# Expert tiles of three sequences computed beside the last sequence's attention, later rows by a second list of four tiles

## The chip, the cores and the metric

The kernel runs on one core of a Trainium2 chip. The metric is the time of one execution on the device in microseconds (us); lower is better. A core has a matrix engine (TensorE, PE in the profile, with its weight loads under PEld), a vector engine (VectorE, DVE), a scalar engine (ScalarE, ACT), a general engine (GpSimd, POOL) and a sync engine (SyncE, SP) that mostly issues DMA transfers. POOL and ACT issue transfers too; a transfer whose addresses come from a tensor (an indirect DMA) is issued by POOL. Each engine works off its own list of instructions in order, and the engines wait for each other by semaphores.

## The reference

Four sequences (B = 4) of 1024 tokens, 256 features each, in float32, go through four blocks, each added onto its input after a layer norm: a gated recurrence, a mixture of 8 experts, causal attention with 16 heads of 64, and a mixture of 32 experts. The change touches the last block, and where the third one ends.

```python
z = jnp.einsum('dvh,bhcv->bcd', W, y) * (math.sqrt(d_embed / d_value) / num_heads)   # end of attention
...
X = x.reshape(-1, D)                                   # 4096 tokens, normalised
logits = (X @ gate_w.T).astype(jnp.float32)
scores = jax.nn.sigmoid(logits)
_, idx = jax.lax.top_k(scores + bias[None, :], K)      # K = 4 of E = 32 experts
w = jnp.take_along_axis(scores, idx, axis=-1)
w = w / jnp.clip(jnp.sum(w, axis=-1, keepdims=True), 1e-12, None)
eid = idx.reshape(-1)
onehot = (eid[:, None] == jnp.arange(E)[None, :]).astype(jnp.int32)
pos = jnp.take_along_axis(jnp.cumsum(onehot, axis=0) - 1, eid[:, None], axis=1)[:, 0]
valid = pos < C                                        # C = 256 rows for each expert
posc = jnp.minimum(pos, C - 1)
xe = jnp.zeros((E, C, D), x.dtype).at[eid, posc].add(jnp.where(valid[:, None], Xrep, jnp.zeros((), x.dtype)))
h = jax.nn.silu(jnp.einsum('ecd,edi->eci', xe, W1)) * jnp.einsum('ecd,edi->eci', xe, W3)
ye = jnp.einsum('eci,eid->ecd', h, W2)
gflat = jnp.where(valid, w.reshape(-1), jnp.zeros((), x.dtype))
yrows = ye[eid, posc] * gflat[:, None]                 # 0 where not valid
out = yrows.reshape(-1, K, D).sum(axis=1)
out = out + jax.nn.silu(X @ sw1.T) * (X @ sw3.T) @ sw2.T     # the shared expert
```

Two things matter. An expert takes only its first 256 entries, in the order of the tokens over all four sequences; later ones count as zero. And `bias` is drawn with a spread of 2, next to scores between 0 and 1, so that nearly every token asks for the same few experts, which the first tokens fill.

## The kernel before, in words

**Slots.** The expert block has 32 x 256 = 8192 slots (`NSLOT`), in 64 slot tiles of 128 rows. `xs_d` in device memory holds one row for each slot (and 128 rows of zeros behind them): the 256 features, their mean and rstd, the four slots that the token has, and the number of the token. `yt_d` holds four result rows for each token. Both are filled with zeros early in attention (`l4_zeros`).

**Routing** (`l4_route(b, h, ...)`, one half of a sequence, 512 tokens): statistics and a layer norm on VectorE, transposes and scores on TensorE, the four best by `max` and `match_replace`, positions by a matmul with a triangular matrix plus the running count (`runs1`), and then 16 indirect scatters (`to_slots`, four k times four tiles of tokens) that POOL issues to write the rows into `xs_d`. For the last sequence only the four scatters with k = 0 are issued at once; the others are kept in the list `late`. `second` keeps, for each half sequence, whether any token has a second valid slot. The first half of the shared expert is computed at the end of `l4_route`, the second half in `l4_shared`, which adds it onto `x`. The gates go to `gates1`.

**Scatters.** The class `Scatters` lets eight indirect scatters be on their way; a reader of the target (`wait`) waits for the last eight sent.

**Attention** is one loop, `run_steps`, over 192 steps: 4 sequences x 8 pairs of heads x 6 steps. The order of the instructions in it is written out by hand (`manual_schedule`): in each step score matmuls, the row minimum on VectorE, exponents on ScalarE (tiles `pe`, eight buffers), transposes and the weighted sum. Other work is woven in by the class `Beside`: a list of jobs, each a Python generator, done one after the other. A job yields "pe" ahead of matmuls, "post" ahead of what reads their result, and "dve" ahead of VectorE work. In a step's three places for side work, matmuls of the job can stand where the list `side` says "beside"; at the end of each step there are 1 to 3 ticks (`TICKS`) for "dve" pieces. While sequence b is in attention, the jobs are: the output projection of sequence b-1 (`l3_out`, matmuls `pz`), the layer norm of sequence b+1, then routing (both halves) and `l4_shared` (both halves) of sequence b-1.

The attention weights behind the first pair of heads are loaded in three transfers of 896 KB each into `wq_t`, `wk_t` and `wv_t`.

**The tail.** Behind the loop come `l3_out` and both halves of `l4_route` of the last sequence; from here on the build's scheduler chooses the order on each engine, under the data dependencies. Then the pool `l4_mid` opens, in space that attention's pools leave, and the expert block is done:

- the count of rows of each expert, `taken1` (which of the 64 slot tiles have rows), a running sum over it (`upto`), and `l4_list(0, 16)`: the numbers of the first 16 occupied tiles, by comparing the running sum with 0 to 15 over 16 x 64 elements; entries beyond the last occupied tile point to the zeros
- a branch (`If`) that issues the `late` scatters if the last sequence has second slots
- `l4_tiles(0, 16)`: for each entry POOL loads the expert's weights (`ew`, 384 KB, by a number read from the list) and SP the tile's rows (`xg`); then normalise (VectorE), transpose (TensorE), copy (ScalarE), two products, SiLU, the third product, a copy, and an indirect scatter of the 128 results to `yt_d` (`to_tokens`)
- a branch that does the other 48 tiles, if more than 16 are occupied
- `l4_shared` of the last sequence
- the results: for each of the 32 tiles of tokens a load `yg` from `yt_d` on SP (`l4_take`) and additions on VectorE (`l4_add`: x + gate * yg); four additions for each tile of the first sequence (all four k), one for the others, 56 in all. Three branches, one for each sequence behind the first, stand between them for second slots. The stores go out on ACT's queue: eight for the first sequence, two for each of the others.

## Time and profile before

| what | value |
|---|---|
| time, median of 7 runs | 2190.59 us (2187.34 to 2197.59) |
| the profiled execution's own time | 2193.18 us |
| its span | 2191.5 us |
| mean granted TensorE clock in it | 0.923 |
| busy share PE / PEld / DVE / ACT / POOL | 86% / 56% / 57% / 44% / 12% |
| moved by DMA | 109.22 MB |
| end of attention (last weighted sums) | 2029.5 us |
| end of `l3_out` of the last sequence | 2057.4 us |
| end of its routing, scatters included | 2092 us |
| first load of slot rows (`xg`) | 2098.36 us |
| first load of results (`yg`) | 2147.69 us |

The profile is one execution, taken by the hardware profiler. Times inside it are microseconds from the start of its span. A row of the timeline has start, length, engine, line and operation; "x16" behind it means that 16 instructions of the kind are drawn together. SPq and POOLq are the times at which an engine's queue issued transfers. The granted clock is the share of full speed at which TensorE was let run in a stretch. Busy shares are averages over the whole span; the stages in the table differ much from them.

### The profile page before, as it was taken

To read this page: it belongs to the slowest core of one execution; us is meant where nothing else is said; L and a number is where in the kernel's file an instruction comes from. 1 tells how busy PE (TensorE), PEld (TensorE's weight loads), DVE (VectorE), ACT (ScalarE), POOL (GpSimd) and SP (SyncE) were. 2 spreads that over 40 slices of the span, in tenths; PEclk is the share of its full clock that TensorE was granted. 3 is DMA by queue.
4 is the path that set the end of the run, shared out by engine and by line. 5 is a ranking of instruction groups with operands and counts; after the bars stand their busy time and mean duration, and the time that the engine had idled before them with its cause. 6 is when DMAs were issued, how large, how long until landed. Compare 5 with 4: busy or idle time off the path is not lost. (4 is left out here: it accounts for less than half of the span.)

```text
span 2191.5 us, 45014 instructions
## 1 busy us (share of the span) xinstructions
PE 1877.4 (86%) x17488; PEld 1221.3 (56%) x17488; DVE 1245.9 (57%) x4059; ACT 965.3 (44%) x2511; POOL 267.7 (12%) x307
## 2 busy tenths in 40 slices
PE   5567699999999999999989799998969988978761
PEld 2435356665656666766646456664546655656541
DVE  6585222244237776647748564774756557656554
ACT  3253122222246666645546453654635345546020
POOL 0233300022012100000020200002020020110040
PEclk9577899999999999999989899998989998989875
DMA  8112211122134423000000000000000000000056
GB/s 326 39 58 73 76 44 49 44 80 77 45 117 146 152 99 122 2 1 2 2 21 2 2 2 2 2 2 2 2 1 2 2 2 2 2 1 2 2 177 212
DMA packets 82351, 109.22 MB, mean 50 GB/s; under 512 B 13646, under 2 KB 71082, under 8 KB 80976
## 3 DMA queue, kind: packets, MB, share of 16 engines
q1 hardware_dynamic: 61632, 73.40, 10.0%
q0 software_dynamic: 15168, 27.05, 4.0%
q10 hardware_dynamic: 5328, 5.78, 0.8%
q8 instruction: 142, 2.33, 0.4%
q14 instruction: 81, 0.66, 0.1%
HBM read 51.75 MB, written 64.77 MB: 53 GB/s over the span
## 5 line engine op out<-in xcount | busy, mean ns | idle before, releaser
L1302 ACT ACTIVATE pe<-ps,nm 128x512 f32<-128x512 f32 (+3 forms) x768 | 438.6, 580 | 263.0 <-DVE nm L1289 252.0
L1323 PE MATMUL pt<-ident,pe 64*128 64x64 f32 x4608 | 254.5, 231 | 91.6 <-issue 31.0
L1359 PE MATMUL pa<-pT,v 128*64 128x128 f32 (+1 forms) x4096 | 325.9, 291 | 3.1 <-issue 3.0
L1323 PEld LDWEIGHTS pt<-ident,pe 64*128 64x128 f32 x4608 | 212.3, 141 | 185.4 <-issue 88.6
L1273 PE MATMUL ps<-k,q 64*128 64x512 f32 (+3 forms) x1536 | 307.4, 507 | 3.6 <-issue 3.5
L1359 PEld LDWEIGHTS pa<-pT,v 128*64 128x64 f32 x4096 | 242.9, 138 | 105.8 <-issue 88.1
L1344 ACT COPY pT<-pt 128x512 f32<-128x512 f32 (+2 forms) x384 | 179.2, 520 | 195.0 <-PE pt L1323 172.3
L604 PE MATMUL ph<-w_t,xgT 128*128 x544 | 257.6, 615 | 7.3 <-DVE desc_C L528 5.8
L1287 DVE TENSOR_REDUCE nm<-ps 128x1 f32<-128x512 f32 x256 | 175.9, 687 | 153.7 <-PE ps L1273 124.8
L849 POOL DMA_INDIRECT xs_d<-x,row_l x104 | 102.6, 987 | 1249.0 <-DVE second L1001 1066.1
L1273 PEld LDWEIGHTS ps<-k,q 64*128 64x128 f32 x1536 | 138.4, 191 | 75.4 <-issue 63.7
L1344 DVE COPY pT<-pt 128x256 f32<-128x256 f32 (+3 forms) x384 | 178.4, 506 | 2.3 <-PE pt L1323 1.3
L1289 DVE CUSTOM_DVE_ANT_0 ps<-ps,mask_a,nm 128x128 f32<-128x128 f32 (+3 forms) x256 | 143.2, 559 | 40.0 <-DVE nm L1287 8.9
L604 PEld LDWEIGHTS ph<-w_t,xgT 128*128 128x128 f32 x544 | 101.0, 197 | 110.7 <-issue 102.3
L1302 ACT ACTIVATION_READ_ACCUMULATOR pe<-ps,nm 128x1 f32 x768 | 153.9, 200 | 0.0
L893 PE MATMUL pq<-l_xT,wq_t 128*64 128x512 f32 x448 | 112.1, 622 | 26.6 <-ACT pe L1302 25.1
L1289 DVE CUSTOM_DVE_ANT_0 ps<-ps,mask_a 128x128 f32<-128x128 f32 (+3 forms) x256 | 119.8, 517 | 23.2 <-PE ps L1273 21.7
L893 PE MATMUL pz<-wo_t,y 128*64 128x256 f32 x1024 | 115.0, 379 | 0.0
L893 PE MATMUL pv<-wv_t,l_xT 128*64 128x128 f32 x1792 | 111.5, 278 | 2.9 <-ACT pe L1302 2.9
L624 PE MATMUL py<-w_t,hidT 128*128 x464 | 109.6, 379 | 0.0
L893 PE MATMUL pk<-l_xT,wk_t 128*64 128x512 f32 x448 | 107.2, 599 | 1.1 <-ACT pe L1302 1.1
L893 PEld LDWEIGHTS pv<-wv_t,l_xT 128*64 128x64 f32 x1792 | 100.7, 140 | 5.6 <-ACT pe L1302 3.6
(370 smaller groups left out, 2201.8 us busy)
## 6 DMA issues: line engine op xcount, KB each, us to landing
yt_d<-zeros SPq DMA_DIRECT2D x32, 512.0 KB
xg<-xe_d SPq DMA_DIRECT2D x68, 129.0 KB
yq_d<-ys SPq DMA_DIRECT2D x68, 128.0 KB
xs_d<-zeros SPq DMA_DIRECT2D x65, 131.5 KB
w_t<-w_dram SPq DMA_DIRECT2D x8, 1024.0 KB
ew<-e_w_dram POOLq DMA_DIRECT2D x16, 384.0 KB
x<-x_in_dram SPq DMA_DIRECT2D x8, 512.0 KB
w_t<-w_dram SPq DMA_DIRECT2D x8, 512.0 KB
```

What stands on the lines that cost most here:

```text
L604: nc.tensor.matmul(pt, xgT[:, c, :], w[:, c, k * H0 : (k + 1) * H0], start=(c == 0), stop=(c == NC_ - 1),)
L624: nc.tensor.matmul(py, hidT[:, c, :], w[:, c, :], start=(c == 0), stop=(c == H0 // P - 1))
L849: i = nc.gpsimd.indirect_dma_start(out=self.out, out_offset=bass.IndirectOffsetOnAxis(ap=idx, axis=0), in_=src, in_offset=None, bounds_che ...
L893: nc.tensor.matmul(out[r], lhsT[:, r], rhs, start=start, stop=stop)
L1273: nc.tensor.matmul(t[:, :n], qs[b, p][rows, i * P : (i + 1) * P], ks[b, p][rows, kc * 512 : kc * 512 + n], start=True, stop=True,)
L1287: nc.vector.tensor_reduce(m[:, 0:1], t, AX.X, ALU.min)
L1289: nc.vector.tensor_tensor_reduce(out=t[:, :n], in0=t[:, :n], in1=mask[:, 512 - n :], scale=1.0, scalar=-LOWEST if kc == 0 else m[:, 0:1], ...
L1302: inst = nc.scalar.activation(pe[:, :n], sps.pop((u, k, par))[:, :n], AF.Exp, bias=ms[u, i, par][:, 1:2], scale=-1.0, accum_out=ls[b, p][: ...
L1323: nc.tensor.transpose(pts[u][r][:, j, par, :], pes[u, k, par][rows, j * P : (j + 1) * P], ident[rows, rows],)
L1344: copy(to, pts[u][r][:, :n])
L1359: nc.tensor.matmul(pas[0][rows, cols], vs[b, p][:, j, rows], pTs[u][:, j, par, a * P :], start=(j == 0), stop=(j == nb - 1),)
```

## The change

1. A new job, `l4_experts_beside`, is appended for `Beside` behind the jobs that run during the last sequence's attention. It waits until the loop has reached the third pair of heads from the end (pair 29 of 0 to 31), by then counts the rows of sequences 0 to 2, makes a list of 12 slot tiles (`NL_A`) and computes these tiles two at a time, in the places that `Beside` has, with results scattered to `yt_d`. What is not done when the loop ends is done behind it, ahead of `l3_out` of the last sequence. Its working space is the buffer of normalised inputs that would belong to a fifth sequence (`room4`), and the attention weights of pairs that are done: `w_pairs[:, 0]` is scratch for the list, `w_pairs[:, 1]` to `[:, 4]` hold expert weights.
2. For that, the attention weights get a new layout, pair by pair, and come in 21 transfers of 128 KB instead of three of 896 KB.
3. `floors` keeps, for each tile that was done, how many rows it had. `owner` holds the number of the last sequence's first result row for these tiles. `over1` says whether more than 12 tiles were occupied.
4. In the tail the list now has 4 entries (`NL_B`), for tiles in which rows came in beyond `floors`. `l4_list` with `first_row` has two more passes to fetch each entry's `owner`, and `l4_rows` has two more operations, which turn away (send out of range) the results of rows that belong to earlier sequences.
5. The loads, additions and stores of sequences 0 to 2 now stand ahead of the tail's first branch and of the four tiles; for sequences 1 and 2 with the first k only. Behind the four tiles and `l4_shared` come eight loads and additions and two stores of the last sequence.
6. The five branches become two, on one flag (`more`): more than 12 tiles at first, more than 4 tiles later, or a second slot in any token behind sequence 0. In the second, all other tiles, additions and stores are done over.
7. SiLU in the expert tiles is worked out with Tanh and two VectorE operations, as the shared expert does it.
8. The buffers of `pe` go from eight to seven. The iotas `tile_t` and `entry` move to the block's setup, early in the kernel.

The new job and its helpers, and the core of the rest (`...` stands for lines left out):

```diff
+NL_A, NL_B = 12, 4
...
+    def l4_keys(flat, name):
+        upto = l4s.tile([P, NL], F32, name=f"upto_{name}", tag="upto")
+        nc.vector.tensor_tensor_scan(upto, ones[:, :NL], flat, 0.0, ALU.mult, ALU.add)
+        key = l4s.tile([P, NL], F32, name=f"key_{name}", tag="key")
+        nc.vector.tensor_mul(key, upto, flat)
+        nc.vector.tensor_scalar(key, key, -1.0, None, ALU.add)
+        return upto, key
+
+    def l4_list(key, j0, n, eq, first_row=None):
+        eq = eq.rearrange("p (n t) -> p n t", t=NL)
+        nc.vector.tensor_tensor(
+            eq, key.unsqueeze(1).to_broadcast([P, n, NL]),
+            entry[:, j0 : j0 + n].unsqueeze(2).to_broadcast([P, n, NL]), ALU.is_equal,
+        )
+        rows = None
+        if first_row is not None:
+            own = l4s.tile([P, 16, NL], F32, name=f"own_{nm}", tag="xT1")[:, :n]
+            nc.vector.tensor_mul(own, eq, first_row.unsqueeze(1).to_broadcast([P, n, NL]))
+            rows = l4s.tile([P, 16], F32, name=f"rows_{nm}", tag="lrows")[:, :n]
+            nc.vector.tensor_reduce(rows, own, AX.X, ALU.add)
+        nc.vector.tensor_mul(eq, eq, tile_t.unsqueeze(1).to_broadcast([P, n, NL]))
+        t = l4s.tile([P, 16], F32, name=f"list_{nm}", tag="list")[:, :n]
+        nc.vector.tensor_reduce(t, eq, AX.X, ALU.add)
...
+        return first, e, slot, rows
+
+    def l4_load(k, lst, xg, w):
+        first, e, slot, rows = lst
+        ev = nc.values_load(
+            e[0:1, k : k + 1], engines=[mybir.EngineType.Pool], min_val=0, max_val=E1 - 1,
...
+        )
+        nc.gpsimd.dma_start(out=w, in_=e_w[bass.ds(ev, 1)].rearrange("o p a i -> p (o a) i"))
+        rv = nc.values_load(
+            first[0:1, k : k + 1], engines=[mybir.EngineType.SP], min_val=0, max_val=NSLOT,
...
+        )
+        to_slots.wait(nc.sync.dma_start(out=xg, in_=xs_d[bass.ds(rv, P), :]).ins)
+
+    def l4_rows(name, xg, slot, row, pool, bufs):
+        nc.vector.tensor_scalar(
+            xg[:, :D], xg[:, :D], xg[:, D : D + 1], xg[:, D + 1 : D + 2], ALU.subtract, ALU.mult
+        )
+        eq = pool.tile([P, K1], F32, name=f"heq_{name}", tag="heq", bufs=bufs)
+        nc.vector.scalar_tensor_tensor(
+            eq, xg[:, D + 2 : D + 2 + K1], slot, choice, ALU.is_equal, ALU.mult
+        )
+        to = pool.tile([P, 1], F32, name=f"to_{name}", tag="to", bufs=bufs)
+        nc.vector.tensor_reduce(to, eq, AX.X, ALU.add)
+        if row is not None:
+            old = pool.tile([P, 1], F32, name=f"old_{name}", tag="old", bufs=bufs)
+            nc.vector.tensor_scalar(old, xg[:, XP - 1 : XP], row, float(FAR), ALU.is_lt, ALU.mult)
+            nc.vector.tensor_add(to, to, old)
+        to_i = pool.tile([P, 1], I32, name=f"to_i_{name}", tag="to_i", bufs=2 * bufs)
+        nc.vector.scalar_tensor_tensor(to_i, to, float(FAR), xg[:, XP - 1 : XP], ALU.add, ALU.add)
+        return to_i
+
+    def l4_experts_beside(sm, ps, tag, w_of, ready):
+        while not ready():
+            yield "dve"
+        room = xtp.tile([P, NC_ * S], F32, name="room4", tag="xT")
...
+        yield "pe"
+        pn = ps.tile([P, E1], F32, name="pn_a", tag=tag)
+        for par in range(2):
+            r = slice(par * DH, (par + 1) * DH)
+            nc.tensor.matmul(pn[r], ones[:, r], runs1[-1][:, NT // 2, :], start=True, stop=True)
+        yield "post"
...
+        yield "dve"
...
+        yield "dve"
...
+        yield "dve"
+        lst = l4_list(key, 0, NL_A, w_of(0).rearrange("p a c m -> p (a c m)"))
+        yield "dve"
...
+        for j in range(2):
+            l4_load(j, lst, xgs[j % 2], weights(j))
+        for j0 in range(0, NL_A, 2):
+            for j in js:
+                yield "dve"
+                tos.append(l4_rows(f"a{j}", xgs[j % 2], lst[2][:, j : j + 1], None, l4s, 1))
+            yield "pe"
...
+            yield "post"
+            nc.scalar.copy(xgT, pt)
+            if j0 + 2 < NL_A:
+                for j in (j0 + 2, j0 + 3):
+                    l4_load(j, lst, xgs[j % 2], weights(j))
+            yield "pe"
...
+            yield "post"
+            nc.scalar.activation(hid, pq[:, :, 0, :], AF.Tanh, scale=0.5)
+            nc.vector.scalar_tensor_tensor(hid, hid, 1.0, pq[:, :, 0, :], ALU.add, ALU.mult)
+            nc.vector.scalar_tensor_tensor(hid, pq[:, :, 1, :], 0.5, hid, ALU.mult, ALU.mult)
+            yield "pe"
...
+            yield "post"
+            nc.scalar.copy(ys, py)
+            for t in range(2):
+                to_tokens(tos[t], ys[:, t, :])
...
-        wq_t = wat.tile([P, NC_, NH * DH - P], F32, name="wq_t")
...
+        w_pairs = wat.tile([P, NP - 1, 3, NC_, P], F32, name="w_pairs")
+        for p in range(NP - 1):
+            for k, src in enumerate((w_q, w_k, w_v)):
+                nc.sync.dma_start(
+                    out=w_pairs[:, p, k], in_=src[:, :, (p + 1) * P : (p + 2) * P]
+                )
...
-                [P, 512], F32, name=f"pe_{b}_{p}_{i}_{kc}_{par}", tag="pe", bufs=8
+                [P, 512], F32, name=f"pe_{b}_{p}_{i}_{kc}_{par}", tag="pe", bufs=7
...
+                    if b == B - 1:
+                        beside.jobs.append(
+                            l4_experts_beside(
+                                sm, ps_s, "s", lambda j: w_pairs[:, j], lambda: at_pair[0] >= B * NP - 3
+                            )
+                        )
...
+        lst = l4_list_b(0, NL_B)
...
+        for t in range((B - 1) * NT):
+            ks = all_k if t < NT else first_k
+            l4_add(t, ks, l4_take(t, ks))
+            if t % (NT // 2) == NT // 2 - 1:
+                l4_store(t // NT, t % NT // (NT // 2))
...
+        with tc.If(more > 0):
+            for t in range(NT, (B - 1) * NT):
+                l4_add(t, other_k, l4_take(t, other_k))
+            l4_clear(0, (B - 1) * NT)
+            for to in late:
+                to_slots(*to)
+        l4_tiles(0, NL_B, lst)
+        for h in range(2):
+            drain(l4_shared(B - 1, h, ps_y, "y"))
+        for t in range((B - 1) * NT, TT):
+            l4_add(t, first_k, l4_take(t, first_k))
+        for g in range(2):
+            l4_store(B - 1, g)
+        with tc.If(more > 0):
+            for t in range((B - 1) * NT, TT):
+                l4_add(t, other_k, l4_take(t, other_k))
+            l4_clear((B - 1) * NT, TT)
+            for j0 in range(NL_B, NL, NX):
+                n = min(NX, NL - j0)
+                l4_tiles(j0, n, l4_list_b(j0, n))
...
```

`l4_tiles`, `l4_hidden` and `l4_out` of the tail stay as they were but for the two products sharing one PSUM tile, Tanh for SiLU, and rows of an entry being prepared two ahead.

## The prediction

> **What bounds the kernel now.** I read the page's first lines, then the stretches of the tail, then the tail in order of time. The page: TensorE holds the span, but its digits fall at the end (8, 7, 6, 1), and the bytes moved rise only in the last two slices.
>
> ```profile
> span 2191.5 us, 45014 instructions
> PE 1877.4 (86%) x17488; PEld 1221.3 (56%) x17488; DVE 1245.9 (57%) x4059; ACT 965.3 (44%) x2511; POOL 267.7 (12%) x307
> ...
> PE   5567699999999999999989799998969988978761
> ```
>
> The chain of waits gives nothing (it is one piece of VectorE, the last additions), so the stretches carry it. Columns: stretch, its length, then busy time (count) of PE, PEld, DVE, ACT, POOL, granted clock, DMA share, GB/s.
>
> ```profile
> 2072.90:2076.70 3.80, 1.32 (x32) 1.09 (x32) 0.89 (x4) 1.04 (x2) 3.04 (x4) 0.79 0.03 3
> 2076.70:2092.00 15.30, 6.75 (x28) 3.90 (x28) 12.37 (x66) 0.87 (x2) 4.11 (x6) 0.72 0.01 2
> 2092.00:2098.00 6.00, 0.00 (x0) 0.00 (x0) 4.32 (x9) 0.00 (x0) 0.14 (x1) 0.51 0.01 0
> 2098.00:2144.00 46.00, 32.12 (x192) 27.25 (x192) 17.55 (x80) 16.49 (x49) 24.37 (x32) 0.83 0.71 212
> 2144.00:2152.50 8.50, 6.22 (x32) 3.34 (x32) 3.05 (x5) 0.00 (x0) 0.00 (x0) 0.64 0.47 155
> 2152.50:2185.50 33.00, 0.00 (x0) 0.00 (x0) 22.70 (x56) 0.00 (x0) 0.00 (x0) 0.52 0.82 280
> ```
>
> The tail is a row of stages with nothing beside them: routing of the last sequence to 2092, the list to 2098, 16 slot tiles to 2144, the shared expert's second half, then 56 additions and stores. The same in order of time (start, length, engine, line, what; in brackets the idle time before):
>
> ```profile
> 1954.02 1.97 PE L893 MATMUL pv<-wv_t,l_xT 128*64 128x128 f32 x32
> ...
> 1956.25 1.03 PE L893 MATMUL sy<-sw_t,sh_l 128*64 128x256 f32 x8
> ...
> 1961.92 0.25 DVE L1203 RECIPROCAL rl<-l 128x16 f32<-128x16 f32 x1
> ...
> 1997.94 0.25 DVE L1203 RECIPROCAL rl<-l 128x16 f32<-128x16 f32 x1
> ...
> 2029.51 27.85 PE L893 MATMUL pz<-wo_t,y 128*64 128x256 f32 x256
> ...
> 2071.63 1.10 POOL L849 DMA_INDIRECT xs_d<-x,row_l  x1 [143.71 <-DVE eq_l L1035]
> ...
> 2076.61 0.21 POOL L1537 IOTA tile_t_i<- 128x64 int32 x1
> ...
> 2098.36 13.22 SPq L1603 DMA_DIRECT2D xg<-xs_d  x16
> ...
> 2147.69 33.73 SPq L1685 DMA_DIRECT2D yg<-yt_d  x32
> ...
> 2151.53 0.48 DVE L1692 SCALAR_TENSOR_TENSOR x<-yg,gates,x 128x256 f32<-128x256 f32 x1 [0.42 <-DMA yg<-yt_d]
> ...
> 2152.53 16.32 DVE L1692 SCALAR_TENSOR_TENSOR x<-yg,gates,x 128x256 f32<-128x256 f32 x40
> ...
> 2184.60 0.89 DVE L1692 SCALAR_TENSOR_TENSOR x<-yg,gates,x 128x256 f32<-128x256 f32 x2 [1.22 <-SPq L1707]
> ```
>
> The reader is to see four prices here: a dense addition is 16.32/40 = 0.41 us; a load of results takes 3.84 us to its first addition; the two reciprocals bound head pair 30 of attention (36.0 us); and TensorE does nothing but `l3_out` for 27.85 us after attention.
>
> **The profiled execution** took 2193.18 us: its span of 2191.54 and 1.64 around it. That is 2.6 above the median of the seven runs (2190.59). I sum against the span and carry the difference to the median.
>
> **Where the twelve tiles land.** The job stands behind `l4_shared` of sequence 2, whose last matmul group (sy) starts at 1961.96 in the trace, the start of pair 30; the condition "pair 29" is met by then and costs no time. From there I counted the places that the step loop gives out: matmul places 2, 2, 0, 1, 1, 2 in a pair's six steps, in the last pair 2, 2, 0, 0, 0, 2 (its steps 3 and 4 have an empty list), and TICKS of 2, 3, 1, 3, 2, 1. The count job takes pair 30 step 1, the loads step 2, tiles 0 and 1 go through in steps 3 to 5, tiles 2 and 3 in steps 0, 1 and 5 of pair 31, and tiles 4 and 5 get as far as their hidden layer. The rest (output of 4 and 5, all of 6 to 11) spills behind the loop, to be drained in front of `l3_out`. So only about half lies beside attention.
>
> **(a) Attention, +11.** For two tiles: 4 transposes at half of the row of 8 (1.09 us at L921), 0.5; 32 half-wide matmuls of the form of pv, 1.97; 8 of the form of sy, 1.03. In the loop are 3, 3 and 2 of these: 1.6 + 5.9 + 2.1 = 9.6. Little of it hides: pairs 16 and 24, with 146 of the pz matmuls each (27.85 x 146/256 = 15.9 us), took 49.8 where pairs without such work take 34.1 (reciprocal to reciprocal). Two more for the list, whose three passes over 768 elements (1.22 x 0.75 each) and some 15 small operations stand on VectorE in one tick, 5.5 us against some 2 us of slack in a step. Less than 8 needs slack that these rows do not have; 15 if the list is not hidden at all. ScalarE's added copies and Tanh lie in its waits (12.7 us for nm from 1962 to 2030). The loads go past nothing: SP issues none then, POOL none; a pair of loads is issued at least one step (some 6 us) before its rows are normalised, against 2.1 us from issue to use at 2098.36. Cover gone, VectorE stands for that load and every score step behind it.
>
> **(b) The spilled tiles, +12.** TensorE: 3, 3 and 4 groups, 1.6 + 5.9 + 4.1 = 11.6, and it is full with `l3_out` until 2057, so they add (lower bound 8, if gaps open). The chain of a tile pair (load, normalise, transpose, copy, hidden, Tanh, two products, output, copy, scatter) is some 8 to 9 us, three of them end within the 40 us. Where a load comes later than its place in the fixed order, TensorE stands: up to 2 us in three rounds, 18 at most. Tiles' 1 us scatters on POOL wait for the copies and only later weights stand behind them.
>
> **(c) Additions of three sequences before the branch, +17.** They take 48 x 0.41-0.48 = 20 to 23 us of VectorE and stand, with 24 loads on SP and 6 stores on ACT, ahead of the branch at which the second list's loads wait. Could they run under `l3_out`, where VectorE is idle? Their tiles belong to `l4_mid`, which takes over the space of attention's pools. In the trace its first instruction, the iota at 2076.61, needs no data, and POOL was idle 143.71 us before 2071.63; yet it comes behind 2072.88, when the last transposes read `xn` of the old pool. I take that as the first moment for the loads; the first addition is 3.8 us later. From 2076.7 VectorE has 12.4 + 4.3 us of routing and list (the second list has 256 elements to a pass instead of 1024 but one pass pair more and the flags, so about the same), plus 20.4: it ends near 2114 instead of 2098. A jump over the branch's body, +1: together +17. Loads keep up: 6 MB at the 280 GB/s of the last row are 22 us, ending before 2099. If the loads may start under `l3_out`, the term is -3; if three buffers of 512 KB make VectorE wait for each, +25.
>
> **(d) Gain, -57.** From the first tile's load at 2098.36 to the end at 2191.54 are 93.2 us. What stays: 4 tiles of which the first needs some 10 us to its copy (2100.48 to 2110.55 in the trace) and the others 2.3 each, last scatter at about +18, landed +20; sy (6.2) under them; 8 loads and 8 additions, +28; store and end, 6.1 as after the last addition now, and 2 for the closing branch: 36. With 30 to 42 for it the gain is 51 to 63. The Silu table load and three branches between additions (waits of up to 3.4 us for SP) go with it.
>
> **Edits at about nothing.** Projection weights in 21 loads instead of 3: issued from 627.4, about 0.5 us each on SP, while pair 1 first reads at 647.09, and its own come first; zero fills behind them on SP wait for 648.7 anyway (without that cover, up to 10 us). Seven exponent buffers instead of eight: the fourth of a step reuses one that the same step's first transposes have read; else 0.3 us a step. Two iotas move into the setup: 0.2 each.
>
> Sum: -57 + 17 + 11 + 12 = **-17**: span 2174.5, time of that execution 2176, on the median's scale **2173**.
>
> [...] Rows: 64 gathers issued by POOL beside VectorE's copies took 947 ns on average, and scatters 987, busy or idle around them; I price POOL's 24 added issues by these, off the path. [...]
> Rows: the three weight loads of 896 KB moved about 400 GB/s. [...]
>
> **Rivals.**
> 1. Additions early: the pool's space is free when attention's weights are done. For: `l3_out` leaves VectorE idle 2.35 us of each 3.45. Against: the late iota. Term (c) becomes -3: **2153**.
> 2. In-order stalls: spilled tiles and additions both wait for DMA longer than planned, terms (b) and (c) at 18 and 21: **2183**. For: VectorE waits 3.2 us for yg in the last loads now. Against: six loads run ahead there.
> 3. Slower: POOL's scatters hold back the other engines. For: while POOL issues 16 of them (1790 to 1810) ScalarE stands 18.33 us before L1015, and 11.3 us at 1911, though TensorE had long finished. Against: with two gathers a step pairs 1 to 3 took 35.9, 35.6 and 35.0. There are six groups of two. If each costs like a batch, 12 us, that is +72: **2246**. It decides at 17/6 = 2.8 us a group.
> 4. It does not do what it says: over 12 tiles are occupied, or a row behind sequence 0 has a second valid slot, and the flagged body does 60 tiles of some 2.8 us, +168: **2341**. Against: the reference's inputs, worked out, fill 10 tiles with three sequences, the last adds rows to one, and no such row has a second slot.
>
> **How the numbers follow.** Forecast 0.43, rival 1 0.13, rival 2 0.17: faster 0.73. Slower 0.21: rival 3 0.15 (0.05 of it below 5 us a group, 2203), rival 4 0.01, other stalls that eat all 17 us 0.05. Same, 0.06, is (b) and (c) near their upper ends with a small gain; about 0.2%, 4.4 us, is what a measurement here tells from no change. The forecast's own range is 2160 to 2184 by its terms; for 8 in 10 I reach to rival 1 below (2150) and into the mild part of rival 3 above (2203).
>
> **What would show it.** Right: 4 tiles behind the last route, xg loads from pair 30 on, pairs 30 and 31 longer by 8 to 15 us together, `l3_out` ending 20 us later, additions dense on VectorE around route's end, under 40 us from the second list's first load to the end. Wrong: gaps of over 3 us on ScalarE or TensorE beside scatters of yt_d (rival 3); additions before route's transposes (rival 1); more than 16 loads of ew (rival 4); a gap in attention in front of the first normalised xg (cover of (a) gone).

## The result: 0.48% slower

The changed kernel takes 2200.22 us (median of 15 runs, 2196.33 to 2209.36) against 2189.92 us for the kernel before on the same chip. The ratio is 1.0048, 95% interval 1.0038 to 1.0058: 10 us slower, where the prediction had 17 us faster. The profiled execution of the changed kernel has a span of 2203.6 us, 12.1 more than before.

The page's first lines of the changed kernel, and its TensorE digits in 40 slices:

```profile
span 2203.6 us, 45192 instructions
PE 1886.6 (86%) x17612; PEld 1227.4 (56%) x17612; DVE 1250.4 (57%) x4095; ACT 962.4 (44%) x2492; POOL 269.2 (12%) x307
...
PE   5567699999999999999989799997979979788762
```

TensorE's busy time rose by 9.2 us and its share is the same. The digits of the last slices (55 us each) say no more than that the work stands elsewhere. The tail has to be read by events. The next view splits the end of the changed kernel into stretches (columns: stretch, length, busy time and count of PE, PEld, DVE, ACT, POOL, granted clock, DMA share, GB/s). The first goes from the reciprocals of pair 29 to attention's last matmul, the second to the first `pz`, the third is `l3_out`, the fourth the routing. The fifth goes on to the first load of the second list, with the additions that remain and the branch, and the last from there to the end.

```profile
1962.40:2057.10 94.70, 77.28 (x939) 55.09 (x933) 57.63 (x183) 47.01 (x129) 8.66 (x12) 0.91 0.17 52
2057.10:2083.80 26.70, 16.32 (x141) 11.36 (x143) 7.60 (x29) 4.71 (x10) 8.56 (x10) 0.78 0.35 103
2083.80:2112.50 28.70, 28.70 (x259) 20.72 (x256) 11.31 (x44) 0.59 (x1) 1.97 (x2) 0.97 0.01 1
2112.50:2149.20 36.70, 18.33 (x133) 11.34 (x132) 30.97 (x157) 3.90 (x8) 8.43 (x8) 0.74 0.35 119
2149.20:2174.30 25.10, 0.00 (x0) 0.00 (x0) 14.68 (x43) 0.00 (x0) 2.22 (x4) 0.50 0.83 268
2174.30:2203.60 29.30, 12.94 (x80) 9.53 (x80) 12.19 (x44) 3.99 (x12) 4.02 (x4) 0.73 0.30 95
```

The first two stages in the trace of before, in the same columns:

```profile
1961.90:2029.60 67.70, 61.52 (x815) 43.23 (x811) 45.03 (x128) 43.07 (x121) 0.00 (x0) 1.00 0.01 2
2029.60:2057.40 27.80, 27.80 (x257) 18.32 (x258) 12.38 (x46) 0.07 (x1) 0.00 (x0) 1.00 0.01 1
```

Set against the same events in the trace of before, with the prediction's terms:

| stage | before | after | difference | predicted |
|---|---|---|---|---|
| start to the reciprocals of pair 29 | 1961.9 | 1962.4 | +0.5 | 0 |
| A: to the end of attention | 67.7 | 94.7 | +27.0 | +11 (a) |
| B: to the end of `l3_out` | 27.8 | 55.4 | +27.6 | +12 (b) |
| C: to the end of the last scatter of routing | 34.8 | 36.7 | +1.9 | C and D: |
| D: to the first load of the tail's list | 6.2 | 25.1 | +18.9 | +17 (c) |
| E: to the end | 93.2 | 29.3 | -63.9 | -57 (d) |

The sum is +12. The tail gave more than it was asked for; A and B took 54.6 us instead of 23.

What VectorE waited for in the changed kernel, first in stage A, then between attention's end and `l3_out` (engine, operation, what it waited for: us in total, times, longest). `nm` holds attention's row minima, `room` the working space of the new job:

```profile
DVE nm L1459 <- PE ps L1445: 10.2, 7, 2.5
DVE to_i_a L1133 <- DMA yt_d<-room,to_i_a: 8.1, 2, 4.5
DVE room L1212 <- ACT room L1211: 7.0, 3, 4.7
DVE room L1117 <- DMA room<-xs_d: 3.8, 2, 3.4
```

```profile
DVE to_i_a L1133 <- DMA yt_d<-room,to_i_a: 12.3, 5, 5.4
DVE room L1117 <- DMA room<-xs_d: 2.9, 3, 1.6
```

The second line was not in any view of before. The tile `to_i` holds the rows to which a scatter writes. It has two buffers for the two tiles of a pair, so the next pair's `to_i` has to wait until the DMA of the last pair's scatter is done with it. In VectorE's list attention's row minima stand behind that one 0.16 us operation, and VectorE began them at 2008.86, when the wait of 4.51 us was over. The place in the timeline (start, length, engine, line, what; idle time before in brackets):

```profile
2005.76 1.04 POOL L859 DMA_INDIRECT yt_d<-room,to_i_a  x1 [26.84 <-ACT room L1219]
...
2008.78 0.16 DVE L1133 SCALAR_TENSOR_TENSOR to_i_a<-to_a,room 128x1 int32<-128x1 f32 x1 [4.51 <-DMA yt_d<-room,to_i_a]
...
2009.30 0.37 ACT L1474 ACTIVATE pe<-ps,nm 128x128 f32<-128x128 f32 x1 [2.26 <-DVE nm L1461]
...
2017.41 3.58 PE L903 MATMUL pea<-room,w_pairs 128*64 128x128 f32 x32 [1.00 <-ACT room L1196]
```

From issue to release the scatter took 3.0 us, and VectorE stood for 4.51. The last line is the second cost of this stall: the same 32 matmuls took 1.97 us at 2059.99. The stretches around it (same columns as above):

```profile
2009.00:2017.00 8.00, 4.93 (x54) 2.99 (x49) 7.46 (x32) 4.83 (x19) 0.30 (x1) 1.00 0.39 115
2017.00:2021.00 4.00, 3.59 (x36) 3.59 (x38) 0.00 (x0) 0.35 (x1) 0.00 (x0) 0.57 0.14 42
2021.00:2028.00 7.00, 6.31 (x84) 4.28 (x82) 5.47 (x13) 5.05 (x14) 0.00 (x0) 1.00 0.00 0
```

While TensorE was fed thinly (4.93 of 8 us) the clock was still 1.00; in the four us behind it was granted 0.57. In stage A as a whole TensorE was busy 77.3 us instead of 61.5 and idle 17.4 instead of 6.2. Of the 15.8 us more of work, the tiles' matmuls at full clock are 10.2 (measured in e1_to_i below, where the stall is gone), and the other 5.6 are slower matmuls.

### The profile page after: what moved, and what is told of

Read it like the earlier page. It is cut to its first block, busy times and chain, and to the rows that moved or that the text cites. A ratio compares the mean times of both kernels' runs of the same rounds, so it can differ in the third digit from the quotient of the medians.

```text
span 2203.6 us, 45192 instructions
## 1 busy us (share of the span) xinstructions
PE 1886.6 (86%) x17612; PEld 1227.4 (56%) x17612; DVE 1250.4 (57%) x4095; ACT 962.4 (44%) x2492; POOL 269.2 (12%) x307
## 5 line engine op out<-in xcount | busy, mean ns | idle before, releaser
L1495 PEld LDWEIGHTS pt<-ident,pe 64*128 64x128 f32 x4608 | 211.6, 141 | 183.8 <-issue 86.3
L1445 PEld LDWEIGHTS ps<-k,q 64*128 64x128 f32 x1536 | 138.0, 191 | 78.1 <-issue 66.3
L903 PE MATMUL pq<-l_xT,w_pairs 128*64 128x512 f32 x448 | 113.4, 628 | 30.2 <-ACT pe L1474 28.9
L903 PE MATMUL pv<-w_pairs,l_xT 128*64 128x128 f32 x1792 | 113.2, 281 | 2.9 <-ACT pe L1474 2.9
L903 PE MATMUL pk<-l_xT,w_pairs 128*64 128x512 f32 x448 | 107.2, 599 | 1.1 <-ACT pe L1474 1.1
L903 PEld LDWEIGHTS pv<-w_pairs,l_xT 128*64 128x64 f32 x1792 | 102.1, 141 | 5.7 <-ACT pe L1474 3.6
```

The source lines that it names most:

```text
L903: nc.tensor.matmul(out[r], lhsT[:, r], rhs, start=start, stop=stop)
L1445: nc.tensor.matmul(t[:, :n], qs[b, p][rows, i * P : (i + 1) * P], ks[b, p][rows, kc * 512 : kc * 512 + n], start=True, stop=True,)
L1495: nc.tensor.transpose(pts[u][r][:, j, par, :], pes[u, k, par][rows, j * P : (j + 1) * P], ident[rows, rows],)
```

## The experiments

The experiments ran on three chips on which the kernel before takes 2062 us, against 2190 on the chip of the profiles above. Where the traces of the chips differ is told under the hardware; why they differ was not found. Each ratio is against the kernel before on the same chip. The changed kernel itself was run there too:

> The changed kernel itself, for a base on the same chip as the three others: as in the first result, 0.4 to 0.6% slower than before (ratio 1.004 to 1.006).

It gave 2075.06 against 2062.57 us, ratio 1.0058 (1.0040 to 1.0076): the change costs about the same there, 12 us. "Changed" below is this run, and what a run's time is less or more than it is the difference of the two ratios, times 2062 us. The stages A to E are measured in each run's profiled execution, by the same events as in the table above. That execution can lie below its run's median, by 7 us in e1_to_i and by 11 in e11_all, so that stages are to be compared with stages and times with times:

| run | ratio to before (95%) | A | B | C | D | E |
|---|---|---|---|---|---|---|
| changed (e0_after) | 1.0058 (1.0040, 1.0076) | 95.1 | 55.1 | 35.8 | 25.3 | 30.3 |
| e1_to_i | 1.0033 (1.0009, 1.0057) | 85.9 | 53.2 | 36.2 | 25.1 | 30.3 |
| e2_behind | 1.0103 (1.0085, 1.0121) | 67.6 | 89.4 | 35.8 | 25.2 | 30.7 |
| e3_ten | 1.0013 (1.0001, 1.0025) | 92.2 | 44.1 | 35.9 | 25.8 | 30.3 |
| e4_weave | 1.0010 (0.9999, 1.0022) | 94.9 | 41.9 | 38.5 | 26.0 | 30.2 |
| e5_early | 1.0011 (0.9998, 1.0024) | 92.2 | 54.9 | 45.6 | 4.3 | 31.9 |
| e7_no_scatter | 1.0041 (1.0022, 1.0060) | 85.5 | 53.9 | 35.8 | 25.6 | 30.5 |
| e8_toi_early | 0.9979 (0.9961, 0.9997) | 85.9 | 54.2 | 45.7 | 4.4 | 30.1 |
| e9_toi_weave_early | 0.9964 (0.9946, 0.9981) | 86.1 | 41.9 | 56.4 | 5.2 | 31.0 |
| e10_toi_adds_woven | 0.9987 (0.9972, 1.0002) | 86.3 | 54.4 | 45.9 | 4.4 | 30.7 |
| e11_all | 0.9958 (0.9941, 0.9976) | 78.1 | 52.5 | 45.2 | 4.4 | 30.5 |
| e12_toi_list | 1.0015 (0.9998, 1.0033) | 82.1 | 54.6 | 36.3 | 24.9 | 30.1 |

The theory drawn from the first result (theory 1 in the expectations): the tiles beside attention cost little more than their matmuls would, if VectorE didn't stand in order for DMA; and behind the loop the tiles are a chain of waits with nothing beside it. Its rivals: POOL's scatters themselves hold the engines back (A, the prediction's rival 3), TensorE's work simply adds up (B), and, for the additions, VectorE is the limit wherever they stand (C).

### A buffer of its own for each tile's rows (e1_to_i)

```diff
-                tos.append(l4_rows(f"a{j}", xgs[j % 2], lst[2][:, j : j + 1], None, l4s, 1))
+                tos.append(l4_rows(f"a{j}", xgs[j % 2], lst[2][:, j : j + 1], None, l4s, 1, NL_A))
...
-        to_i = pool.tile([P, 1], I32, name=f"to_i_{name}", tag="to_i", bufs=2 * bufs)
+        to_i = pool.tile([P, 1], I32, name=f"to_i_{name}", tag="to_i", bufs=to_bufs or 2 * bufs)
```

> The twelve tiles' index tiles to_i get twelve buffers instead of two; nothing else changes. Theory 1 (VectorE's in-order waits): the seven waits of VectorE for the scatters of yt_d, 20.4 us in the changed kernel, go. The 8.1 us that lie inside attention come off in full, of the 12.3 behind it up to half is taken over by the next wait of the chain (ys, hid and xgT have one buffer, xg two): 14 to 20 us less, 2180 to 2186. Rival A (POOL itself holds the other engines back while it issues scatters, my rival 3): the buffer changes nothing, 2198 to 2202. Rival B (the tiles' work on TensorE simply adds up): no change, 2198 to 2202.

Stage A fell by 9.2 us, somewhat more than the 8.1 that theory 1 had for it. TensorE was idle 5.1 us less there (12.9 instead of 18.0) and busy 4.2 us less, with the same matmuls. The four other runs with twelve buffers and this list have 85.5 to 86.3 us in stage A. Of the runs with two buffers and tiles beside attention, three have 94.7 to 95.1, and e3_ten and e5_early 92.2, in which TensorE kept its full clock behind the first of the two stalls; so some 3 of the 9.2 us depend on how the clock falls (an estimate from these stages). The time fell by 5.2 us, and the two intervals overlap, where 14 to 20 were expected. The missing part is behind the loop. VectorE's waits there, between attention's end and `l3_out`, are now:

```profile
DVE room L1117 <- DMA room<-xs_d: 9.5, 4, 4.5
DVE room L1212 <- ACT room L1211: 6.8, 2, 6.1
```

The 12.3 us for `to_i` were taken over whole, mainly by the wait for the next rows' load: 25.4 us from attention's end to the first `pz`, against 26.1. In the loop nothing takes over, and TensorE's clock comes back: the third pair's 32 matmuls took 1.97 us.

```profile
1882.52 1.97 PE L903 MATMUL pea<-room,w_pairs 128*64 128x128 f32 x32 [1.00 <-ACT room L1196]
```

### The same without ten of the twelve scatters (e7_no_scatter)

```diff
-            for t in range(2):
-                to_tokens(tos[t], ys[:, t, :])
+            if j0 == NL_A - 2:
+                for t in range(2):
+                    to_tokens(tos[t], ys[:, t, :])
```

> As e1_to_i, but of the twelve scatters of the first list only the last two are issued (the results of ten tiles are left out of the output). Rival A (POOL's scatters themselves hold the engines back) would make attention's end come at least 5 us earlier than in e1_to_i (from the reciprocals of pair 29 to the end 85.9 us there). Theory 1 (only VectorE's wait for them cost time): no change at this place, 85 to 87 us; behind the loop at most the additions' loads start earlier.

Stage A is 85.5 us, against 85.9 with all scatters. Rival A is out: issuing a scatter costs the other engines nothing here that can be seen; the wait for its end did. This chip is not the one of the first result, but stage A of the changed kernel is 94.7 us there and 95.1 in e0_after.

### All tiles behind the loop (e2_behind)

```diff
-                                sm, ps_s, "s", lambda j: w_pairs[:, j], lambda: at_pair[0] >= B * NP - 3
+                                sm, ps_s, "s", lambda j: w_pairs[:, j], lambda: behind[0]
...
```

> The tiles' job starts only behind the loop: no tile beside attention, all six pairs of tiles behind it. Theory 1 (a chain of waits, 8.4 us for a pair of tiles behind the loop; 27 us for the list and two pairs beside attention): attention from the reciprocals of pair 29 to its end takes 68 us as before, 24 to 27 less than changed; the list and two more rounds behind it are 8 + 17 = 25 more: the same time as the changed kernel within 4 us, so attention hides nothing of its share. If attention did hide half of the tiles' work there (what my prediction took from the pairs of heads, 11 us for list and four tiles), it is 14 us slower than the changed kernel.

Attention is back at 67.6 us (67.7 before, so that seven buffers of `pe` and the new layout of the weights cost nothing there), and the list and six pairs of tiles take 61.6 us in front of `l3_out` (89.4 less 27.8). So the list and the two pairs that the changed kernel finishes beside attention save 34.3 behind the loop and cost 27.5 in it: attention hides 7 us by the profile, 9 by the times. Expected were at most 4, or 14 if it hid half; it is between the two, nearer to the first.

### Ten tiles, and weaving (e3_ten, e4_weave)

```diff
-NL_A, NL_B = 12, 4
+NL_A, NL_B = 10, 4
...
```

> The first list has 10 tiles instead of 12 (the inputs fill 10; the two left out hold zeros). Theory 1 (behind the loop the tiles are a chain of waits, one round for each pair of tiles): one round less, by the distance of the last scatters of the changed kernel (2068.2, 2075.2, 2085.0) 7 to 10 us, and a sixth of the list's three passes, 0.5 us: 2190 to 2193. Rival B (TensorE's work adds up): one group of transposes and products, 0.54 + 1.97 + 1.03 = 3.5 us, and the list: 2196.

The time is 9.3 us less than changed, and stage B 11.0 less. That is a round of the chain (8.3 us on average in e2_behind) and more, not the 3.5 us of its matmuls: rival B is out for this stage.

e4_weave keeps the twelve tiles and emits one group of `l3_out` behind each of the job's groups on TensorE, in an order fixed by hand:

```diff
-        while beside.jobs or beside.job is not None:
-            beside.step()
-        drain(l3_out(B - 1, ps_s, "s"))
+        last = l3_out(B - 1, ps_s, "s")
+        next(last)
+        with tc.manual_schedule():
+            while beside.jobs or beside.job is not None:
+                pe = beside.next == "pe"
+                beside.step()
+                if pe:
+                    next(last, None)
+                    beside.step()
+                    next(last, None)
+            drain(last)
```

> The rest of the tiles' job behind the loop is emitted by hand in turn with l3_out of the last sequence: one of its 8 groups of pz behind each of the job's groups on TensorE. Theory 1: the 27 us between attention's end and the first pz hold some 12 us of work on TensorE and 15 of waiting; the waiting is filled: 12 to 15 us less, 2185 to 2188. Rival B: TensorE's work adds up wherever it stands, no change, 2198 to 2202.

Stage B fell by 13.2 us, as expected, and the time by 9.9 (stages C and D gave 3.4 back). TensorE's waits from attention's end to the first `pz` in the changed kernel:

```profile
PE pya L903 <- DVE room L1213: 7.4, 4, 3.4
PE pea L903 <- ACT room L1196: 2.2, 3, 0.7
PE pta L1194 <- DVE room L1117: 0.9, 1, 0.9
```

and in e4_weave from attention's end to the end of `l3_out`:

```profile
PE pta L1194 <- DVE room L1117: 2.7, 4, 0.8
PE pta L1194 <- PE pz L903: 1.8, 2, 0.9
PE pya L903 <- DVE room L1213: 0.5, 1, 0.5
```

The rounds got longer (15 us instead of 8, and the last scatter comes behind `l3_out`), but `l3_out` is done meanwhile, and the granted clock was 1.00 over the whole 41.9 us.

### The list in four ticks (e12_toi_list)

In the changed kernel the list stands on VectorE in one piece, and TensorE and ScalarE wait for the minima behind it:

```profile
1970.44 0.95 DVE L1077 TENSOR_TENSOR w_pairs<-key_a,entry 128x768 f32<-128x768 f32 x1
1971.42 0.96 DVE L1087 TENSOR_TENSOR w_pairs<-w_pairs,tile_t 128x768 f32<-128x768 f32 x1
1972.42 0.95 DVE L1089 TENSOR_REDUCE list_key_a<-w_pairs 128x12 f32<-128x768 f32 x1
...
1975.39 0.69 ACT L1474 ACTIVATE pe<-ps,nm 128x512 f32<-128x512 f32 x1 [5.45 <-DVE nm L1461]
...
1976.22 1.12 PE L903 MATMUL pq<-l_xT,w_pairs 128*64 128x512 f32 x2 [5.13 <-ACT pe L1474]
```

The edit makes `l4_list` a generator with a `yield "dve"` behind each of its passes, on top of e1_to_i.

> As e1_to_i, and the first list's three passes and the small operations behind them stand in four ticks of the loop instead of one. Theory 1: the 5.1 us in which TensorE and ScalarE stood for the list (ScalarE 5.45, TensorE 5.13 before L1474 and L903 in the changed kernel) shrink to 1 to 2 us: from pair 29's reciprocals to attention's end 82 to 83 us instead of 85.9; the job begins its tiles up to three ticks later, which may push a piece behind the loop (up to 2 us back). In all 1 to 4 us less than e1_to_i.

Stage A is 82.1 us, 3.8 less than in e1_to_i. The times point the same way, within their intervals (1.0015 against 1.0033, on different chips). With it stage A can be added up: 67.7 before, 10.2 us of the tiles' matmuls, 3.8 for the list, 9.2 for `to_i` and the clock, and some 4 that were not taken apart.

### The additions ahead of `l3_out` (e5_early, e8_toi_early)

```diff
+        def l4_early():
+            for t in range((B - 1) * NT):
+                ks = range(K1) if t < NT else range(1)
+                yg = mid.tile([P, S], F32, name=f"yge_{t}", tag="qkv"[t % 3])
...
+        drain(l4_early())
         drain(l3_out(B - 1, ps_s, "s"))
...
-        for t in range((B - 1) * NT):
-            ks = all_k if t < NT else first_k
-            l4_add(t, ks, l4_take(t, ks))
```

The result tiles lie in the buffers of q, k and v of attention instead of the pool that opens late.

> Loads, additions and stores of sequences 0 to 2 are emitted ahead of l3_out of the last sequence, with result buffers in the pool of attention (the buffers of q, k and v) instead of the tail's pool. Theory 1: in l3_out VectorE is idle 2.35 us of 3.45, some 19 us in 8 groups, so that nearly all 20 us of additions hide there, and the skipped branch no longer waits for stores issued just before it (5.8 us from the last addition to the first load of the second list): 18 to 25 us less, 2175 to 2182. Rival C (the additions only move: they delay l3_out's own additions and the routing behind them on VectorE): less than 5 us, 2195 to 2200.

Stage D fell from 25.3 to 4.3 us, and C rose from 35.8 to 45.6. The time is 9.7 us less than changed, about half of what was expected. VectorE's time in `l3_out` is not free for all of it: the first addition comes 8.4 us behind the first `pz`, when the last scatters have landed and been loaded, and then the 48 stand ahead of five of `l3_out`'s own eight additions and of the routing's statistics.

> Twelve to_i buffers, and the additions of sequences 0 to 2 emitted ahead of l3_out. The two alone gave, by their profiles, some 7 us inside attention (pairs 30 and 31 at 46.9 and 32.2 us instead of 49.1 and 36.7) and some 12 us from l3_out's end to the second list. Theory 1: they lie at different places and add up, 17 to 20 us less than changed, that is 6 to 10 us below before.

Both edits together take 16.3 us less than changed, which is 4.3 below before. Alone they took 5.2 and 9.7 less, so they do add up, a little under the forecast.

### Weaving or placing by hand on top (e9_toi_weave_early, e10_toi_adds_woven)

> As e8_toi_early, and the rest of the job is emitted in turn with l3_out's groups. Theory 1: another 13 us at l3_out (the weaving alone ended l3_out 41.9 us behind attention instead of 55), of which additions that then come later give back 5 to 10: 20 to 28 us less than changed, 10 to 16 below before. Rival C (VectorE is the limit from l3_out on): no less than e8_toi_early.

Stage B fell by 12.3 us and C rose by 10.7. With its longer rounds the woven job sends its last scatter 49 us behind attention's end instead of 28, so that the first addition comes 55 us behind it instead of 34, when `l3_out` is over, and the additions then stand beside the routing. The time is that of e8_toi_early within the intervals, as rival C had it.

e10_toi_adds_woven emits the additions by hand, six behind each group of `l3_out` from the second on, with the loads of results six tiles ahead:

```diff
+        with tc.manual_schedule():
+            next(last)
+            next(early)
+            for i in range(NT):
+                next(last, None)
+                next(last, None)
+                for k in range(6 if i else 0):
+                    next(early, None)
+        drain(early)
```

> As e8_toi_early, but the additions are emitted by hand, six behind each of the groups 1 to 7 of l3_out, so that l3_out's own additions no longer stand behind them; the last six come behind it. Theory 1: in e8_toi_early 45.7 us lie between l3_out's end and the last scatter of the routing, in the changed kernel 35.8: the 10 us are l3_out's additions and statistics that stood behind 48 additions. They come back but for the six that are left over (2.5 us): 36 to 40 us at this place, 6 to 9 us less than e8_toi_early, ratio to before 0.993 to 0.996.

This missed. `l3_out`'s own additions were nearly on time (the last 2.1 us behind `l3_out`'s end), but stage C stayed at 45.9 us. The 48 additions ran from 19.5 us ahead of `l3_out`'s end to 12 behind it, 31 us for 23 us of work, with waits of VectorE of 4.2 us for their loads. The routing's last statistics came 12 us behind `l3_out`'s end, against 0.5 in the changed kernel. That the order among additions and routing behind the loop is what is left to win there is argued, not tried.

### These additions, the list in four ticks and two overlapped stages for the tiles (e11_all)

The job gets two sets of buffers; in the order of TensorE the next pair's transposes stand between a pair's products and its output, and rows are loaded two pairs ahead:

```diff
+        for i in range(NJ):
...
+            if i + 1 < NJ:
+                yield from rows(i + 1)
...
+            if i + 1 < NJ:
+                yield from turned(i + 1)
...
+            load_w(i + 2)
```

> As e10_toi_adds_woven, the list in four ticks, and the tiles' job in two overlapped stages (the next pair's normalising and transposes stand ahead of this pair's output, two buffers for each tile, loads of rows two pairs ahead). Theory 1: behind the loop a pair of tiles takes 8.4 us as a chain and 3.5 to 5 us when it is bound by TensorE: 8 to 13 us less between attention's end and l3_out, 2 to 4 us less inside attention: ratio to before 0.985 to 0.991. If the rounds stay at 8 us, the chain is not what I took it for (then POOL's two loads and two scatters of a pair, some 3.3 us, or the loads' landing set the round).

It took 2051.55 against 2061.74 us, ratio 0.9958 (0.9941 to 0.9976). That is faster than both kernels, by less than expected. A and B together are 130.5 us, against 140.8 in e10_toi_adds_woven. A pair takes 6.0 us on average behind the loop instead of 8.2, but the order starts later in the loop, so that five pairs instead of four end behind it. The starts of the scatters show rounds of 4.4, 9.4 and 4.4 us (the one behind them has 5.6):

```profile
1908.11 1.04 POOL L859 DMA_INDIRECT yt_d<-w_pairs,to_i_a  x1 [0.50 <-DVE to_a L1139]
...
1912.47 1.04 POOL L859 DMA_INDIRECT yt_d<-w_pairs,to_i_a  x1 [0.51 <-DVE heq_a L1135]
...
1921.86 1.04 POOL L859 DMA_INDIRECT yt_d<-w_pairs,to_i_a  x1 [0.93 <-ACT w_pairs L1260]
...
1926.30 1.01 POOL L859 DMA_INDIRECT yt_d<-w_pairs,to_i_a  x1 [1.48 <-ACT w_pairs L1260]
```

What sets the long round was not settled.

## Why the prediction was wrong, step by step

**The sum.** The prediction had -17 us and the profile shows +12. The 29 us between them are +16.0 at (a), +15.6 at (b), +3.8 at (c), -6.9 at (d) and +0.5 ahead of pair 29.

**Where the tiles land: right.** Two pairs of tiles were scattered inside attention (from 2005.8 and 2043.9), and the third was in its hidden layer when attention ended, as counted out; eight tiles were finished behind it.

**(a) Attention, +11: failed, +27.0.** Its price for the matmuls, 9.6, was right (10.2). The list was sized at two us, though the figures given there, 5.5 against 2 of slack, leave 3.5, and it measured 3.8; 9.6 and two are also 11.6 and not 11. What was missing altogether is `to_i`. The prediction asked what stands behind POOL's scatters on POOL ("only later weights") and what covers the loads; it did not ask who waits for a scatter's end. Each `to_i` that a scatter's DMA reads is written next by VectorE, in front of attention's minima. That cost 9.2 us by e1_to_i, 5.1 of them idle time of TensorE and 4.2 its slower matmuls. The cover of the rows' loads held for two of the three pairs; for the third VectorE waited 3.4 us.

**(b) The spilled tiles, +12, at most 18: failed, +27.6.** The step that failed is that the spilled matmuls stand beside `l3_out`, so that only their time on TensorE counts. The 8 to 9 us for a pair were right (8.3 in e0_after and e2_behind, 8.5 in the first profile), but `l3_out` came behind all of them, and the chain stood alone: 26.7 us with TensorE busy 16.3, at a granted clock of 0.78. With the order made by hand (e4_weave) the stage costs +14.1, near the term. Nothing in the trace of before showed that `l3_out` would be drawn forward; the term's upper end should have been three to four whole rounds, some 30 us. Why the scheduler left `l3_out` behind the job was not looked into.

**(c) Additions, +17: right but for the branch.** It measured +18.9 at D and +1.9 at C, 20.8 together. The late pool was read rightly: the first load came directly behind the routing's last transposes.

```profile
2126.95 0.95 PE L931 MATMUL pt_l<-ident,xn_l 128*128 128x128 f32 x4 [0.81 <-DVE xn_l L919]
...
2128.04 15.28 SPq L1720 DMA_DIRECT2D yg<-yt_d  x15
```

Inside it the branch was under-sized: it was put at 1 us, an estimate that no row of before shows, and 5.8 lie between the last addition's end (2168.48) and the second list's first load. What SP waited for stands below, under the hardware.

**(d) The gain, -57: right in kind, -63.9.** 29.3 us stayed instead of 36, 0.7 below the lower bound that was given: the last scatter came 13.4 us behind the first load instead of 18. How much of the gain comes from fewer tiles, from Tanh for SiLU and from fewer branches was not taken apart.

**The rivals.** Rival 2, in-order stalls, was the mechanism, with its price cut off too low (18 and 21, where B alone was 28) and without the stall inside attention. Rival 1 fell by the two lines above, rival 3 by e7_no_scatter, rival 4 by the 16 loads of expert weights in the tail and the loop together (twelve and four).

**Edits at nothing** held: up to pair 29 the two kernels differ by 0.5 us, with 21 weight loads and seven buffers. The 21 loads were issued within 15 us (627.69 to 642.68), and pair 1 first read at 646.21.

**POOL's issues.** They were priced by rows of before, 947 ns on average for a gather and 987 for a scatter, and put off the path. The scatters of the job took 983 to 1147 ns, median 1032, but VectorE worked beside only one of the twelve. In e0_after it worked beside 100 of the 104 scatters of the routing, and these took 982 to 1339 ns, mean 995. That the issues themselves cost the other engines nothing that can be seen is shown by e7_no_scatter: it leaves out ten scatters, and stage A stays within 0.4 us. What stood on the path was the wait for a scatter's end, under (a).

## What to carry to other kernels

When work is woven into an engine's fixed order, follow each buffer that a DMA reads to the engine that writes it next: with as many buffers as one round uses, here two, VectorE stood 8.1 us for the DMA's end inside attention, and what stood behind it on its queue waited too. Work that spills behind a loop counts as its whole chain, here 8.3 us for a pair of tiles, not as its matmuls, here 3.5, unless its order beside other work is made by hand (13.2 us less at stage B in e4_weave). And work taken off the tail is not won until the place to which it goes has been priced with its waits: here the tail gave 64 us and the new places took 76.

## What the runs showed of the hardware

**TensorE's granted clock fell to 0.50 behind thin feeding.** Between 2009 and 2017 no gap on TensorE was longer than 1.23 us, and it was busy for 4.93 of 8 us; then the clock was granted at 0.57 on average for four us, in the record at 0.50 for 3.41 us, and the 32 matmuls there took 3.58 us instead of 1.97. Behind the first 300 us the traces of both kernels on the first chip, of e0_after and of e1_to_i have 70 falls from full to half clock, and 66 of the 70 stretches at half clock last 3.41 us or a multiple of it. In the 3.41 us ahead of each fall TensorE was busy for at most 2.2 us. Counted back from there in steps of 3.41 us, every step that left the clock full had TensorE busy for at least 1.4 us. Between 1.4 and 2.2 us both occur in these traces; what decides there was not found.

**At the skipped branch SP waited 7.9 us, for stores among others.** SP reached its branch at 2165.4, before the last additions, and issued the next load at 2174.27. In between it waited, by the trace's waits of SP:

```profile
SPq L1837 <- SPq L1837: 7.9, 6, 1.7
```

In the trace SP waits there, behind its branch, for eight semaphores in turn, four of them those of stores. The stores issued at 2167.0 to 2168.5 were still under way, and SP passed their semaphores at 2170.54, 2171.91 and 2173.39. Why it waits for these eight is not shown. With the stores early (e5_early) stage D is 4.3 us.

**One chip stood for batches of scatters, three did not.** On the chip of the first result the six pairs of heads during which POOL issues 16 scatters of the routing took 56.4 to 60.9 us in the changed kernel; on the chip of e0_after 39.9 to 43.2, with batches of the same length (20.4 us), and the traces from the two other chips (e1_to_i, e7_no_scatter) show 39.9 to 43.2 too. ScalarE's longest wait in the batch that starts at 1787.6 on the first chip is for nothing that the profile shows ("remote"):

```profile
ACT sh_l L1025 <- remote: 18.4, 1, 18.4
```

In the same batch on the other chip the same instruction waits for its matmul only:

```profile
ACT sh_l L1025 <- PE s_l L903: 2.1, 1, 2.1
```

Over the six pairs that is 99 of the 129 us between the two spans of the changed kernel. The two scatters at a time of the new job did not show it: stage A is 94.7 us on the one and 95.1 on the other. What makes the chips differ was not found.
